# Where a scan batch routes its tokens: one batch later, or within the same batch

## The chip, the cores and the metric

The kernel runs on one core of a Trainium2 chip. The metric is the device time of one execution in microseconds (us), the median of several runs. Five engines work side by side, each through its own queue in a fixed order: PE (TensorE, matrix products), DVE (VectorE), ACT (ScalarE), POOL (GpSimd) and SP (SyncE, which here only issues transfers). An instruction whose input is not ready holds up all that stands behind it in its queue. Data move between the chip's memory (HBM) and the on-chip memory (SBUF) by DMA transfers; PE writes to PSUM, of which there are eight banks.

## The reference, cut to what matters

The input x has 8 batches of 512 tokens of 256 numbers each. Four layers follow one another, each added to x: a scan layer, a mixture of experts, an attention layer, and the same mixture again. The change touches the scan layer and the first mixture:

```python
xi = silu(x @ Win + bin_)                 # scan layer, x normalised
h = h * 0.9 + xt[:, :, None] * Bp         # a state for each channel, token after token
y = einsum('bij,ji->bi', h, Cp) + Dp * xt
x = x + y @ Wout + bout
...
scores = sigmoid(x @ router_w.T)          # mixture, x normalised again, 16 experts
# of four groups of four experts the best two by their two best scores; then the best four experts
tw = tw / tw.sum() * 2.5
x = x + sum of tw * expert(x) over the four experts + shared_expert(x)
```

## The kernel before, in words

Everything is float32. The work has four stages: the **scan stretch** (scan layer, routing and the shared part of the first mixture, `stretch(Scan())`, L1489), the routed experts of the first mixture (`routed`, L1494), the attention stretch with the second mixture's routing and shared part (`stretch(Attention())`, L1498), and the second mixture's routed experts (L1567). Between the two kinds of stage lies memory: routing sends each token's normalised row, with its four expert numbers and weights, to four places of a sorted table `xg` in HBM, and the routed stage reads that table block by block.

In a stretch, batch b of the layer runs beside other work for other batches: the routing of batch b-1 (its x is final when its layer is done), the rest of the routing of batch b-2, the shared experts of batch b-2, and the norm and transposes of batch b+1. The batches are the steps of the loop at L1410; batch 0 has its own start (`first_two`, L1387).

For the scan layer, `main` (L521) works through four **columns** of 128 channels. For each: four PE instructions into `pz_s` (L529), a sigmoid on ACT (L538), a product on DVE (L539), the scan on DVE (L541), a product with Dp on ACT (L542), a sum on DVE (L545). Then come four tiles of the output projection `py_s` on PE (L483), which DVE adds to x in pairs (L492). The shared experts (L1045) give four pairs of products `pg_m` (L1060), each with a sigmoid on ACT (L1078) and two products on DVE (L1079, L1080), and then sums `pd_m` (L1089).

The **routing** of a batch (class `Route`, L579, and `choices`, L650) is a chain through all engines:

- norm: statistics on DVE (L441, L442), the reciprocal root on POOL (L461), the normalised rows on DVE (L466), written into a tile `sorted_m` of which there are two. An `iota` on POOL (L591) writes token numbers into it. In the scan stretch the rows of a route stand behind the last weights (L741) of the route before it (`past`, L601).
- scores: transposes on PE into `pt_m` (L403), copies on ACT to `xT_m` (L405), products with the router's weights `pl_m` (L627), a transpose on DVE (L638), a sigmoid on ACT (L642).
- choices, five steps on DVE (L652 to L697, a chain of small instructions): the best groups, the best four experts, and a table `sel_m` of them.
- prefix products: `sel_m` times a triangle and times ones on PE into `pr_m` (L705, L706), which count how many earlier tokens chose each expert; DVE adds the counts of earlier batches (L708, L710, L716).
- places: DVE picks the four places of each token (L722, L728); then the weights (the same lines on the scores, L738 to L741).
- scatters: 16 indirect transfers on POOL (L755), each of which sends 128 rows of the tile to their places. ACT casts the places to whole numbers two scatters at a time (L752), pinned behind what ACT was given before.

**The order.** Each piece of work is a generator that yields between its steps. `beside` (L346) merges pieces: it always advances the one that is least far along, as a share of its own length. `timed` (L362) gives a piece that has no length of its own a list of **places**, one for each step, as shares of the batch (0 its start, 1 its end). The result is the program's order. The compiler's scheduler then builds each engine's queue from it: among the instructions that it takes to be ready, the one that comes first in the program's order goes first. In the trace PE's queue follows the places: batches 3 to 6 have the same order of products.

The places of the scan stretch (L500) are, for the routing of batch b-1 within batch b: norm statistics 0.08 to 0.2, rows 0.32 to 0.4, transposes at 0.48 and 0.52, logits from 0.61, choices 0.71 to 0.97. Its prefix products, places and weights come in batch b+1 at 0.1, 0.14 and 0.18, its 16 scatters there from 0.22 to 0.86 (L1427). The last batch of the loop (batch 7, L1432 to L1443) has a list of its own, in which route 6 goes as far as its first four scatters (`SENT`), beside the 16 scatters of route 5 (0.22 to 0.66). Route 7 is worked out behind the loop (L1467 to L1477), beside the other 12 scatters of route 6, and its last scatters with the block tables behind that.

Of the kernel before, what the change touches and what calls it, by code (L numbers as in the profile page):

```python
# [19 lines left out]
NT = T // P  # L20
# [11 lines left out]
EG, TKG, TK = 4, 2, 4  # L32
# [29 lines left out]
SENT = 4  # L62
# [6 lines left out]
PICKS = 5  # L69
# [11 lines left out]
def tile_hybrid_block(  # L81
# [67 lines left out]
    def rows_of(part, b: int):  # L149
        return part[b * T : (b + 1) * T, :].rearrange("(t p) d -> p t d", p=P)  # L150
# [57 lines left out]
    def load_shared():  # L208
        nc.sync.dma_start(out=sg_sb, in_=sh_gate_w.rearrange("(p k) f -> p k f", p=P))
        nc.sync.dma_start(out=su_sb, in_=sh_up_w.rearrange("(p k) f -> p k f", p=P))  # L210
        nc.sync.dma_start(out=sd_sb, in_=sh_down_w.rearrange("(k p) d -> p k d", p=P))
# [150 lines left out]
    def timed(steps, *places):  # L362


        def scaled():
            now = 0
            for place in places:
                yield place - now
                now = place
                next(steps)  # L370
            for _ in steps:
                pass

        return Piece(1, scaled())

    def spread(first: float, last: float, many: int):
        return [first + (last - first) * k / many for k in range(many)]

    def some(steps, many: int):

        for _ in range(many):
            yield next(steps)

    def issue(piece):
        for _ in piece.steps:
            pass
# [85 lines left out]
    def kb4(name: str):  # L472
        return work.tile([P, NT, D], FP, tag="kb4", name=name, bufs=KB)
# [21 lines left out]
    class Scan:  # L495
# [1 line left out]
        early = 0  # L497


        norms, scores, choose = (0.08, 0.2, 0.32, 0.4), (0.48, 0.52, 0.61, 0.66), (0.71, 0.97)  # L500
        last_rows, last_scores = (0.26, 0.33), (0.43, 0.46)

        def load(self, b: int):
# [611 lines left out]
    class Attention:  # L1115
        mixture, ahead, copies, turns = 1, 2, by_both, (0.65, 0.85)
        early = 2
        norms, scores, choose = (0.0, 0.12, 0.2, 0.28), (0.29, 0.45, 0.55, 0.6), (0.66, 0.95)
        last_rows, last_scores = (0.2, 0.28), (0.35, 0.38)

        def end(self):
# [222 lines left out]
    def stretch(layer):  # L1344


        i = layer.mixture
        xT, xn, made, routes, sends = {}, {}, {}, {}, []

        def norm(b: int, first: bool = False):  # L1350
            def place():
                xn[b] = kb4(f"xn_{i}_{b}")
                return xn[b]

            return normed(b, f"l{i}_{b}", place, first, first)

        def turn(b: int, copies=layer.copies):
            if i == 1 and b >= layer.ahead:
                return by_shares(lambda: xn.pop(b), f"l{i}_{b}", lambda xnT: xT.update({b: xnT}), True)
            return turned(lambda: xn.pop(b), f"l{i}_{b}", lambda xnT: xT.update({b: xnT}), copies)  # L1360

        def project(b: int):
            made[b], piece = layer.project(b, xT.pop(b))
            return piece

        def store(b: int):
            nc.sync.dma_start(out=rows_of(parts[i][0], b), in_=x_tiles[b])

        def experts(b: int):
            return shared_experts(i, b, lambda: routes.pop(b).held["xnT"], i == 1)  # L1370

        for b in range(layer.ahead):
            if b < layer.early:
                if b in unturned:
                    issue(Piece(0, unturned.pop(b)))
                xT[b] = ready.pop(b)
            else:
                layer.load(b)
                first = i == 0 and b == 0
                issue(Piece(0, norm(b, first)))  # L1380
                issue(Piece(0, turn(b, by_both if first else layer.copies)))
                if first:
                    load_shared()
            if b == 0:
                issue(project(b))

        def first_two():  # L1387

            layer.load(1)
            issue(Piece(0, norm(1, True)))  # L1390
            for _ in range(2):
                pending.pop(0)()
            main = layer.main(0, made.pop(0))
            issue(Piece(0, some(main.steps, NI)))
            issue(Piece(0, turn(1)))
            issue(project(1))
            second = layer.main(1, made.pop(1))
            issue(Piece(0, some(second.steps, NI)))
            issue(main)
            return Piece(second.columns - NI * KD * T, second.steps)  # L1400

        def start_route(b: int):
            routes[b] = Route(i, b, layer.copies)
            store(b)
            return routes[b]

        begun = None
        if layer.mixture == 0:
            begun = first_two()
        for b in range(1 if begun else 0, B):  # L1410
            pieces = [begun or layer.main(b, made.pop(b))]
            begun = None
            nxt, last = b + layer.ahead, b == B - 1
            fill = []
            if layer.ahead > 1 and not last:
                fill.append(project(b + 1))
            if b > 1:
                shared_sum = experts(b - 2)
                if last:

                    each = shared_sum.columns // 12
                    rest = Piece((12 - HELD) * each, shared_sum.steps)

                    many = HELD * each if layer.mixture else HELD * each * 3 // 2
                    shared_sum = Piece(many, some(shared_sum.steps, HELD))
                fill.append(shared_sum)
                pieces.append(timed(sends.pop(), 0.1, 0.14, 0.18, *spread(0.22, 0.66 if last else 0.86, NT * TK)))  # L1427
            if fill:
                pieces.append(behind(*fill))
            if b > 0:  # L1430
                r = start_route(b - 1)
                if last:  # L1432
                    pieces.append(timed(r.norm(), *spread(0.0, 0.12, NT), *spread(*layer.last_rows, NT)))
                else:
                    first, then, rows, full = layer.norms
                    pieces.append(timed(r.norm(), *spread(first, then, NT), *spread(rows, full, NT)))
                sends.append(r.rest)
                if last:
                    pieces += [
                        timed(r.scores(), *layer.last_scores, *spread(0.5, 0.56, NT)),  # L1440
                        timed(some(r.rest, PICKS), *spread(0.57, 0.67, PICKS - 1), 0.76),
                        timed(some(r.rest, 3 + SENT), 0.79, 0.81, 0.83, *spread(0.85, 1.0, SENT)),
                    ]  # L1443
                else:
                    pieces += [
                        timed(r.scores(i == 1), *layer.scores[:2], *spread(*layer.scores[2:], NT)),
                        timed(some(r.rest, PICKS), *spread(*layer.choose, PICKS)),
                    ]
            if nxt < B:
                added = layer.load(nxt)  # L1450
                if added is not None:
                    pieces.append(timed(added, 0.24, 0.28))
                pieces += [
                    timed(norm(nxt), *spread(0.32, 0.44, NT), *spread(0.56, 0.64, NT)),
                    timed(turn(nxt), *layer.turns),
                ]
            issue(beside(*pieces))
            if layer.ahead == 1 and nxt < B:
                issue(project(nxt))
            if i == 0 and b == 2:  # L1460
                for make in pending:
                    make()
        layer.end()

        r = start_route(B - 1)  # L1467
        chain = 3 + PICKS
        issue(
            beside(  # L1470
                behind(rest, experts(B - 2)),
                timed(r.norm(by_vector=True), *spread(0.0, 0.05, 2 * NT)),
                timed(sends.pop(), *spread(0.0, 0.5, NT * TK - SENT)),
                timed(r.scores(), 0.2, 0.22, *spread(0.28, 0.33, NT)),
                timed(some(r.rest, chain + 8), *spread(0.36, 0.68, chain), *spread(0.7, 1.0, 8)),
            )
        )  # L1477
        table = []
        issue(
            beside(  # L1480
                experts(B - 1),
                timed(r.rest, *spread(0.0, 0.5, NT * TK - 8)),
                timed(blocks(i, table), 0.03, 0.14, 0.26, 0.38),
            )
        )
        return table

    with banks_of(one=8):
        table = stretch(Scan())  # L1489
        wqkv_sb, wo_sb = load_attention_weights()  # L1490
# [136 lines left out]
```

## Time and profile before

| | us |
|---|---|
| median of 10 runs | 1686.69 |
| lowest and highest run | 1680.57, 1690.44 |
| the profiled execution | 1694.76 |
| its span, first to last instruction | 1693.0 |
| busy PE, DVE, ACT, POOL in the span | 1607.1, 1163.4, 750.2, 758.9 |
| scan stretch, batches 2 to 7 of its loop | 59.5 to about 300 |
| its tail, up to the last shared-expert product | to 351.4 |

The profile is of one execution. Batch b of the scan stretch can be found by its first products `pz_s`: batch 2 starts at 59.5 us, batch 3 at 101.8, batch 4 at 140.8, batch 5 at 179.9, batch 6 at 218.9, batch 7 at 257.9. In a timeline line the columns are start, duration, engine, source line, operation, output<-inputs, shapes and count; a bracket at the end is the time for which the engine was idle before, and what ended it. Names have their numbers left out: `sorted_m` is that of any route. A matmul in float32 shows as two records.

### The profile page before, as it was taken

What the parts mean: (1) busy time and instruction counts of PE and PEld (TensorE: products, weight loads), DVE (VectorE), ACT (ScalarE), POOL (GpSimd) and SP (SyncE); (2) the same over time, 40 slices, a digit from 0 to 9 for tenths busy, and PEclk for the clock granted to TensorE, in tenths of its full rate; (3) what the DMA queues carried; (4) which work ended last, traced back from release to release, by engine and by line L of the source; (5) the groups of instructions that cost most, each with busy time, mean ns of one, the idle gap of its engine ahead of it and who ended that gap; (6) DMA issues with size and microseconds to landing.
All of it is one profiled execution on the core that took longest, in us unless ns stands there. A gap on an engine that the chain in (4) does not pass through costs nothing.

```text
span 1693.0 us, 34302 instructions
## 1 busy us (share of the span) xinstructions
PE 1607.1 (95%) x9996; PEld 1162.2 (69%) x9996; DVE 1163.4 (69%) x3693; ACT 750.2 (44%) x1494; POOL 758.9 (45%) x656
## 2 busy tenths in 40 slices
PE   6899998999999999999999999999999999999993
PEld 3566665589999999963344444444457999999993
DVE  7888888545666766647887877877754766666662
ACT  3232232135555555544544344344314555555551
POOL 3355555635554655530031431422452555455563
PEclk8999999999999999999999999999999999999997
DMA  5345423547776776541324234232544777677776
GB/s 164 121 162 178 147 86 104 192 95 105 107 103 102 109 103 102 75 79 38 88 80 122 90 92 123 78 101 71 171 169 94 109 103 101 102 133 125 126 128 180
DMA packets 278382, 192.95 MB, mean 114 GB/s; under 512 B 166992, under 2 KB 259952, under 8 KB 278192
## 3 DMA queue, kind: packets, MB, share of 16 engines
q1 hardware_dynamic: 224528, 114.68, 26.9%
q0 software_dynamic: 51984, 72.09, 23.9%
q10 hardware_dynamic: 1680, 3.93, 0.6%
q8 instruction: 85, 1.39, 0.4%
q14 instruction: 105, 0.86, 0.2%
HBM read 87.36 MB, written 103.23 MB: 113 GB/s over the span
## 4 chain that ended last, share of the span: by engine, by line
PE 39%; DVE 7%; DMA 3%; issue 2%; POOL 1%; ACT 0%; SPq 0%; DVEq 0%; POOLq 0%; ACTq 0%
PE ph L953 15%; PE pyr L984 7%; PE ps_a L1198 4%; PE pg_m L1060 3%; PE po_a L1233 3%; PE pd_m L1089 2%; PE pq_a L1143 2%; PE pv_a L1161 2%; PE py_a L483 1%; POOL xg L755 1%; DMA part<-rows 1%; DMA xg<-sorted_m,slots_m 1%; DVE w_all L1212 1%; DVE w_all L1220 1%; DMA sum<-part 1%
## 5 line engine op out<-in xcount | busy, mean ns | idle before, releaser
L994 POOL DMA_INDIRECT part<-rows x272 | 425.5, 1564 | 358.0 <-ACT rows L993 213.5
L755 POOL DMA_INDIRECT xg<-sorted_m,slots_m x256 | 259.5, 1014 | 310.9 <-issue 76.0
L953 PEld LDWEIGHTS ph<-rows,gate 128*128 128x128 f32 x2160 | 279.9, 192 | 29.3 <-ACT rows L936 18.8
L953 PE MATMUL ph<-rows,gate 128*128 128x128 f32 x2160 | 292.4, 279 | 0.0
L953 PE MATMUL ph<-rows,up 128*128 128x128 f32 x2160 | 285.9, 275 | 0.0
L984 PE MATMUL pyr<-w_all,rows 128*128 x1088 | 278.9, 380 | 0.0
L926 DVE COPY up<-w_all 128x512 f32 x270 | 119.1, 442 | 219.0 <-PE ph L953 202.2
L953 PEld LDWEIGHTS ph<-rows,up 128*128 128x128 f32 x2160 | 263.7, 193 | 0.0
L926 ACT COPY gate<-w_all 128x512 f32 x270 | 166.3, 618 | 115.6 <-PE ph L953 108.6
L984 PEld LDWEIGHTS pyr<-w_all,rows 128*128 128x128 f32 x1088 | 187.0, 192 | 14.4
L993 ACT ACTIVATE rows<-pyr,gain 128x256 f32<-128x256 f32 x272 | 128.7, 473 | 80.8 <-PE pyr L984 61.0
L961 ACT ACTIVATE rows<-ph 128x256 f32<-128x256 f32 x272 | 104.3, 384 | 123.4 <-PE ph L953 106.7
L1209 ACT ACTIVATE w_all<-ps_a 128x1024 f32<-128x1024 f32 x128 | 124.4, 1020 | 54.3 <-PE ps_a L1198 51.1
L963 DVE TENSOR_TENSOR rows<-ph,rows 128x256 f32<-128x256 f32 x272 | 115.1, 423 | 45.4 <-ACT rows L961 41.2
L1198 PE MATMUL ps_a<-w_all 32*128 32x384 f32 (+3 forms) x1024 | 125.5, 483 | 9.5 <-ACT w_all L1209 8.7
L964 DVE TENSOR_TENSOR rows<-ph,rows 128x256 f32<-128x256 f32 x272 | 115.3, 424 | 26.3 <-PE ph L953 1.7
L1060 PE MATMUL pg_m<-xT_m,su_sb 128*128 128x512 f32 x256 | 125.4, 612 | 0.0
L1089 PE MATMUL pd_m<-sd_sb,act_m 128*128 128x256 f32 x512 | 122.2, 383 | 2.8 <-DVE act_m L1076 2.0
L1060 PE MATMUL pg_m<-xT_m,sg_sb 128*128 128x512 f32 x256 | 123.6, 606 | 0.0
L1089 PEld LDWEIGHTS pd_m<-sd_sb,act_m 128*128 128x128 f32 x512 | 95.4, 190 | 28.0 <-issue 6.7
L1198 PEld LDWEIGHTS ps_a<-w_all 32*128 32x128 f32 x1024 | 49.6, 190 | 78.3 <-issue 29.9
L1060 PEld LDWEIGHTS pg_m<-xT_m,sg_sb 128*128 128x128 f32 x256 | 47.4, 194 | 58.6 <-issue 50.4
(222 smaller groups left out, 2067.5 us busy)
## 6 DMA issues: line engine op xcount, KB each, us to landing
rows<-xg SPq DMA_DIRECT2D x712, 32.0 KB
rows<-xg SPq DMA_DIRECT2D x94, 134.0 KB
part<-x SPq DMA_DIRECT2D x16, 512.0 KB
part<-ys_m SPq DMA_DIRECT2D x14, 512.0 KB
sum<-part SPq DMA_DIRECT2D x13, 512.0 KB
w_all<-in_L_ffn_gate_w_dram SPq DMA_DIRECT2D x24, 256.0 KB
w_all<-in_L_ffn_up_w_dram SPq DMA_DIRECT2D x24, 256.0 KB
w_all<-in_L_ffn_down_w_dram SPq DMA_DIRECT2D x24, 256.0 KB
```

Of the source, the lines that this page charges most:

```text
L755: nc.gpsimd.indirect_dma_start(out=xg[i], out_offset=bass.IndirectOffsetOnAxis(ap=slots[:, at : at + 1], axis=0), in_=rows[:, t, :], in_of ...
L926: copy(here, w_all[:, bass.ds(held[n][0] + half * KD * F, KD * F)])
L953: nc.tensor.matmul(ph[s][:, f * P : (f + 1) * P], lhsT=both[s][:, k * F + f * P : k * F + (f + 1) * P], rhs=rows[:, ROW + k * P : ROW + (k ...
L963: nc.vector.tensor_mul(act, ph[0], act)
L964: made = nc.vector.tensor_mul(act, ph[1], act)
L984: nc.tensor.matmul(py, lhsT=act[:, f * P : (f + 1) * P], rhs=w_all[:, bass.ds(w + 2 * KD * F + f * D, D)], start=(f == 0), stop=(f == KF - 1),
L993: nc.scalar.mul(y, py, gain[:, TK : TK + 1])
L994: nc.gpsimd.indirect_dma_start(out=parts[i][n % 2], out_offset=bass.IndirectOffsetOnAxis(ap=rows[:, D + 2 * TK : D + 2 * TK + 1].bitcast(U ...
L1060: made = nc.tensor.matmul(dst, lhsT=w[:, k, f * P : (f + 1) * P], rhs=xnT[:, k, :], start=(k == 0), stop=(k == KD - 1),)
L1089: nc.tensor.matmul(py[:, j, :], lhsT=acts[n][:, f, t * P : (t + 1) * P], rhs=shared[n][3][:, f, :], start=(n == 0 and f == 0), stop=(n == ...
L1198: nc.tensor.matmul(ps[j // 2][:, j % 2, col : col + n], lhsT=k_sb[w][r, o, c * P : (c + 1) * P], rhs=q_sb[r, o, c * P : T], start=True, st ...
L1209: nc.scalar.activation(es[two], ps[two][:, :, 0:cols], AF.Exp, scale=ATT_SCALE)
```

## The change

The routing of batch b-1 is moved forward within batch b, and three more steps of it and four scatters are put into that batch. The last batch of the loop, the work behind the loop and the attention stretch keep their places; in the last batch only what is left of route 5 changes.

| step of route b-1 | before | after |
|---|---|---|
| norm statistics | 0.08 to 0.2 | 0.0 to 0.12 |
| rows | 0.32 to 0.4 | 0.2 to 0.28 |
| transposes | 0.48, 0.52 | 0.34, 0.38 |
| logits | 0.61 to 0.66 | 0.46 to 0.51 |
| choices | 0.71 to 0.97 | 0.56 to 0.76 |
| prefix products, places, weights | 0.1, 0.14, 0.18 of batch b+1 | 0.8, 0.83, 0.86 |
| scatters 1 to 4 | 0.22 to 0.38 of batch b+1 | 0.9 to 1.0 |
| scatters 5 to 16 | 0.38 to 0.86 of batch b+1 | 0.0 to 0.6 of batch b+1 |

Where batch b+1 is the last, its scatters ran from 0.22 to 0.66 before, and the remaining 12 run from 0.0 to 0.45 after.

```diff
-        norms, scores, choose = (0.08, 0.2, 0.32, 0.4), (0.48, 0.52, 0.61, 0.66), (0.71, 0.97)
+        norms, scores, choose = (0.0, 0.12, 0.2, 0.28), (0.34, 0.38, 0.46, 0.51), (0.56, 0.76)
+        places, sends, rest = (0.8, 0.83, 0.86), (0.9, 1.0, SENT), (0.0, 0.45, 0.6)
...
+        places, sends, rest = (), (0.0, 0.0, 0), (0.22, 0.66, 0.86)
...
-                pieces.append(timed(sends.pop(), 0.1, 0.14, 0.18, *spread(0.22, 0.66 if last else 0.86, NT * TK)))
+                first, end, full = layer.rest
+                first_steps = () if layer.places else (0.1, 0.14, 0.18)
+                left = NT * TK - layer.sends[-1]
+                pieces.append(timed(sends.pop(), *first_steps, *spread(first, end if last else full, left)))
...
-                        timed(some(r.rest, PICKS), *spread(*layer.choose, PICKS)),
+                        timed(
+                            some(r.rest, PICKS + len(layer.places) + layer.sends[-1]),
+                            *spread(*layer.choose, PICKS),
+                            *layer.places,
+                            *spread(*layer.sends) if layer.places else (),
+                        ),
```

The second `places, sends, rest` line is the attention layer's, which keeps what it had.

## The prediction

> **What bounds the kernel now.** I read the windows view first, cut at the batches of the scan stretch (the first line is batch 2, then 3, 6, 7 and the tail). Columns: stretch, then busy time of PE, weight loads, DVE, ACT and POOL, the granted clock, DMA share and GB/s.
>
> ```profile
> 59.50:101.80 42.30, 40.16 (x149) 24.74 (x149) 35.78 (x125) 11.26 (x26) 21.15 (x23) 0.96 0.45 155
> 101.80:140.80 39.00, 38.16 (x149) 24.07 (x148) 34.43 (x113) 11.96 (x27) 20.36 (x23) 1.00 0.45 156
> 218.90:257.90 39.00, 38.16 (x149) 24.07 (x148) 31.42 (x87) 11.97 (x27) 22.04 (x24) 1.00 0.24 84
> 257.90:300.00 42.10, 35.11 (x129) 20.19 (x128) 32.58 (x112) 10.76 (x29) 22.64 (x25) 1.00 0.40 133
> 300.00:351.40 51.40, 51.27 (x196) 31.40 (x196) 24.14 (x86) 9.38 (x20) 26.73 (x28) 1.00 0.46 151
> ```
>
> PE bounds the stretch: batches 3 to 6 take 39.0 us for 38.2 us of matmuls. Only 0.84 us a batch is to be had there, 2.1 in batch 2, 7.0 in batch 7. The waits of PE from 59.5 to 300 us say for what (total, times, longest):
>
> ```profile
> PE pt_m L403 <- DVE sorted_m L466: 6.1, 7, 1.1
> PE pr_m L705 <- DVE sel_m L697: 3.5, 1, 3.5
> PE pl_m L627 <- ACT xT_m L405: 1.4, 1, 1.4
> ```
>
> All are the routing that the change moves. The pt_m waits are 1.09 and 1.05 us in batch 2, 0.84 in each of batches 3 to 6, 0.64 in batch 7; the other two are batch 7's. The timelines of batch 7 and after:
>
> ```profile
> 272.91 1.03 PE L403 MATMUL pt_m<-ident,sorted_m 128*128 128x128 f32 x3 [0.64 <-DVE sorted_m L466]
> 277.65 0.43 PE L627 MATMUL pl_m<-xT_m,rw_sb 128*32 128x128 f32 x8 [1.41 <-ACT xT_m L405]
> 287.47 0.43 PE L705 MATMUL pr_m<-sel_m,tri 128*128 128x64 f32 x2 [3.47 <-DVE sel_m L697]
> 300.00 1.82 PE L403 MATMUL pt_m<-ident,sorted_m 128*128 128x128 f32 x8 [1.48 <-DVE sorted_m L466]
> ```
> ```profile
> 276.31 0.72 ACT L542 ACTIVATE xi_s<-xi_s,d_sb 128x512 f32<-128x512 f32 x1 [3.08 <-DVE state_s L541]
> 277.02 0.57 ACT L405 COPY xT_m<-pt_m 128x512 f32<-128x512 f32 x1
> ```
> ```profile
> 273.35 1.05 POOL L755 DMA_INDIRECT xg<-sorted_m,slots_m  x1 [11.79 <-ACT slots_m L752]
> ...
> 292.56 0.97 POOL L755 DMA_INDIRECT xg<-sorted_m,slots_m  x1 [0.30 <-DVE x L492]
> ```
> ```profile
> 299.50 1.41 DVE L466 TENSOR_SCALAR sorted_m<-x,mv_m,rstd_m 128x256 f32<-128x256 f32 x4 [2.74 <-DMA xg<-sorted_m,slots_m]
> ```
>
> The reader is to see two chains. The transposed copies stand in ACT's queue behind the product of column 3, which waits for DVE's scan. And route 5's 16 scatters start 15 us late and run to 293.5 us; their landing holds the tile that route 7's rows need, so PE waits until 300.0.
>
> **What is moved.** For routes 0 to 5: the prefix products (4 PE records, 0.4 us), 14 DVE instructions of L708 to L741 (batch 4's rows sum to 3.4 us), 2 of 8 casts on ACT (0.18 each) and 4 of 16 scatters (0.96 plus 0.30 of issue each on POOL) go ahead of the batch's end; the other 12 scatters start at 0. Nothing is added. No SP instruction moves. Norms, transposes, logits and choices go 0.12 to 0.2 of a batch forward within it. Work on each engine is the same, so only waits can change.
>
> **Batch 7 and tail.** (1) The 3.4 us of route 5's DVE work, at 264.0 to 272.2 in this trace, is gone. The rows of route 6, which had to follow its last instruction, come at about 269 and the 0.64 wait goes. (2) The scan of column 3, ended at 276.3, is then held by its own chain alone: products done 270.4, sigmoid 0.9, L539 0.7, scan 1.1, so 273.1. The copies no longer stand behind it, PE gets to pl_m at 275.6 rather than 276.2, and the 1.41 goes. (3) The 3.47 stays: from pl_m's end (279.5) to sel_m's (287.4) DVE runs a chain of 7.9 us, which starts 2.05 earlier, as PE does. (4) Twelve scatters at 1.27 from 257.9 end at 273, landed (2.7 median, 6.5 longest) by 280. Route 7's rows then wait for their rstd alone, 296.8 - 2.05 = 294.7, are done by 296.2, and PE's sum products before them end at 298.5 - 2.05 = 296.5: the 1.48 goes. Sum: 0.64 + 1.41 + 1.48 = **3.5 us off**. What is late next: from 300 to 351 PE is idle for 0.13 us, and everything behind hangs on PE; route 7's scatters (321 to 341.8) follow that route's chain and move with it. Bounds: 7.0 if the 3.47 goes too, 1.5 if only the landing does.
>
> **Batches 3 to 6.** I lay out a new batch with the start-to-start times of the rows (a column of pz_s or half pair of pg_m 1.72, a tile of py_s or pd_m 1.73, half of pt_m 0.47, pl_m 0.57, pr_m 0.4), t from the batch's start, in order of the places: pt_m at 15.5, xT wanted for pl_m at 18.1, pr_m at 31.7 (place 0.8 ties with the third tile of py_s, which goes first), end at 38.2. The rows no longer follow a gain of the same batch; rstd comes by 2.7 (L460 ends 0.4 into batch 5, a scatter may be ahead for 1.27, the power takes 1.04), so they are done by 8 to 10, between columns 0 and 1, and the 0.84 goes. But the transposes stand 3.1 us nearer to column 3: its products end at 13.7, its scan at 16.7, the product L542 at 17.5, so a copy behind it ends at 18.1 to 18.7. I take 0.5 us of new wait at pl_m; 0 if the copies stand in front, 1.4 (batch 7's row) if DVE is late again. At pr_m: pl_m ends at 19.2, sel_m followed 10.0 us later in batch 5 (205.8 to 215.8), one pair of shared experts (1.25) now falls into that chain, so 30.5, before 31.7: nothing, 3.47 (batch 7's row) at worst. After pr_m, DVE has 3.4 + 0.6 + 1.4 us for 6.5 of PE, so gains are ready about at the batch's end; casts and scatters wait for nothing longer than that. Their POOL queue then holds rstd for one scatter at most (1.27), which the 15.5 of pt_m hides; without that cover PE would wait the same 1.27. Sum per batch -0.84 + 0.5 = -0.3; **four batches, 1.2 us off**, from 3.4 off to 16 on.
>
> **Batches 1 and 2.** DVE, not PE, bounds these: it is hardly idle from 53.8 to 82.4. Route 0's 3.4 us now stand in front of batch 2's columns instead of between them, so the sum up to column 3's scan (end 79.4) is the same, and 1.0 more with three rows pulled in front: 80.4. Behind it stand L542 (0.8) and a copy (0.6), so pl_m starts at about 82.0, while PE is there at 59.5 + 18.1 + 0.4 = 78.0. The 2.14 of pt_m go, 4.0 at pl_m come. Then pl_m and two half pairs (0.57 + 3.43) bring PE to the first py_s at 86.0; it was 86.3. If the copies stand in front of the product, py_s starts at 82.1, when column 3 is done: 4.2 off. pr_m in batch 1, if it is queued ahead of batch 2's columns, stops PE up to 5 us for sel_m (64.6), most of it under DVE's work: 1.5 on at most. I take **0**, from 4.2 off to 3.2 on (1.5 + 1.7, next).
>
> Clock: in batch 2 the granted clock reads 0.50 at 82 to 84 us after the waits of 1.09 and 1.05; four matmuls of pg_m take 3.24 there against 1.88. With pt_m's second half that is 1.70 us. After batch 7's 3.47 the clock stays 1.00. I keep the 1.70 in batch 2, as a wait stays there. [...]
>
> **The sum.** -3.5 - 1.2 + 0 = -4.7 us on the profiled execution's 1694.8 (span 1693.0 and 1.8 around it): 1690.1. That execution is 8 us above the median of the runs, 1686.7; I carry the difference over: **1682.0**. A measurement can tell about 0.2% (3.4 us) from no change.
>
> **Rivals.**
> - All waits of batches 2 to 6 go and none comes: 4 x 0.84 + 2.14 + 1.70 + 3.5 = 10.7 off, 1676.0. For it: DVE is idle for 4.6 us (39.0 - 34.4) or more in batches 3 to 6. Against: up to column 3 of batch 2 it has next to none.
> - Slower: PE stops at pr_m and pl_m in batches 2 to 6, since both now follow close behind what they need in queues that are fixed. For it: batch 7 already has choices and pr_m in one batch, and pays 3.47 and 1.41. Against: there PE has few other products between them. It decides where the chain from pl_m to sel_m is over 12.5 us, or column 3's scan over 1 us late. At 1.5 us for each wait: 5 x (3.0 - 0.84) = 10.8 on, less 3.5: 7.3 on, 1694.0.
> - It does not do what it says, or the gain is eaten: the compiler's order goes by what it takes to be ready, so the queues may hardly change, or the 3.5 are lost at the first block of the routed stage, where PE waits 0.92 and 1.70 and the clock is 0.50 from 356 to 359. About 1 off, 1685.7.
>
> **How the numbers follow.** Forecast 0.46 (own range 1679 to 1685.5; 0.36 of it faster by over 0.2%, 0.10 within); all waits go 0.14 (faster); eaten 0.14 (within); slower 0.26 (0.21 over 0.2%, 0.05 within). Together 0.50, 0.29, 0.21. Range 1675 to 1694: it takes in both outer rivals; batches 3 to 6 at their worst lie outside.
>
> **What would show it.** Right: route 5's last scatter of the loop near 273 us on the old time scale, no DMA in front of route 7's rows, no pt_m wait in batches 3 to 6, a short one at pl_m, a long one at pl_m in batch 2, pr_m unwaited except in batch 7. Wrong: waits at pr_m in every batch, batches over 39.0 us, or a tail that starts as late as before.

## The result, and the profile after

The changed kernel takes **1707.3 us** (median of 17 runs, 1701.99 to 1713.09), the kernel before 1688.0 us (median of 62 runs, 1680.57 to 1698.69): a ratio of 1.0116, 95% interval 1.0104 to 1.0128. The change makes the kernel 19 us slower, where I forecast 4.7 us faster; the time lies outside the range.

The profiled execution of the changed kernel took 1705.3 us; its span of 1703.6 is 10.6 us above that of before. The execution profiled of before is 7 us above its median and that of after 2 us below, so the two profiles show only a part of the 19 us. Up to the end of the tail the changed kernel is 15.0 us later (366.4 against 351.4 us). Of these 15.0 us, 13.7 are left at the first product of the attention stretch (748.9 against 735.3), 11.5 at the last routed stage's first (1294.9 against 1283.4) and 10.6 at the end. The change touches none of these later stages, and no run here shows why they are shorter in this execution.

The windows view of the changed kernel, cut at its own batches: 2, 3, 4, 6, 7 and the tail. Columns as in the prediction: stretch, then length, busy time of PE, weight loads, DVE, ACT and POOL, the granted clock, DMA share and GB/s.

```profile
63.40:102.86 39.46, 39.08 (x150) 24.43 (x150) 35.73 (x107) 11.59 (x28) 22.07 (x21) 0.97 0.38 134
102.86:145.05 42.19, 39.02 (x149) 24.32 (x148) 34.02 (x114) 11.65 (x27) 23.16 (x24) 0.96 0.44 149
145.05:185.73 40.68, 37.80 (x149) 23.86 (x148) 33.09 (x96) 11.67 (x27) 21.94 (x24) 1.00 0.39 136
226.42:269.80 43.38, 40.54 (x150) 24.89 (x148) 31.07 (x88) 11.67 (x27) 22.04 (x24) 0.92 0.22 75
269.80:315.81 46.01, 38.48 (x125) 22.61 (x124) 31.30 (x100) 10.25 (x27) 24.66 (x26) 0.89 0.34 115
315.81:366.40 50.59, 50.46 (x197) 31.06 (x195) 23.32 (x84) 9.38 (x20) 24.77 (x25) 1.00 0.47 155
```

Batch 2 starts 3.9 us later than before (63.4 against 59.5) and is 2.8 shorter; batches 3 to 6 took 39.0 each and take 42.2, 40.7, 40.7 and 43.4; batch 7 is 3.9 longer, the tail 0.8 shorter. Sum: 3.9 - 2.8 + 10.8 + 3.9 - 0.8 = 15.0. The first term depends on the execution: a1 and a3 below, whose order on PE is the same up to there, have the same wait of 4.6 us, but start batch 2 at 66.4 and 64.9. At 50 to 55 us, at the end of batch 1, the clock reads 1.00 in the changed kernel's profile and 0.66 in that of before; two records of py_s take 0.60 us there in the changed kernel, and 1.06 in a1.

The waits of PE in the changed kernel from 55 to 330 us (total, times, longest):

```profile
PE pl_m L628 <- ACT xT_m L405: 16.0, 6, 4.1
PE pr_m L706 <- DVE sel_m L698: 8.1, 2, 4.6
```

The pt_m waits, 7.6 us in 8 places before, are gone, as the prediction said. In their place PE waits 16.0 us for transposed copies, once in each of batches 2 to 7, and 4.6 more for a selection. The places of the two, and batch 7 and the tail that answer to the prediction's lines (timeline of PE: start, duration, engine, line, operation, output<-inputs, elements, count, and in brackets the idle time before it and what ended it):

```profile
62.53 0.66 PE L706 MATMUL pr_m<-sel_m,tri 128*128 128x64 f32 x2 [4.61 <-DVE sel_m L698]
...
63.41 3.15 PE L530 MATMUL pz_s<-xT_l,w_scan 128*128 128x512 f32 x4
```
```profile
290.40 0.43 PE L628 MATMUL pl_m<-xT_m,rw_sb 128*32 128x128 f32 x8 [4.06 <-ACT xT_m L405]
...
301.80 0.69 PE L706 MATMUL pr_m<-sel_m,tri 128*128 128x64 f32 x2 [3.47 <-DVE sel_m L698]
...
315.81 1.10 PE L403 MATMUL pt_m<-ident,sorted_m 128*128 128x128 f32 x8
```

The first is route 0's prefix product at the end of batch 1: 4.61 us of nothing, then batch 2's first column, at a clock that reads 0.50 from 63.4 to 65.4 us (3.15 us against 1.88). In batch 7 the pl_m wait has grown from 1.41 to 4.06 and the 3.47 at pr_m is unchanged; in the tail the 1.48 before route 7's transposes is gone.

**Where the 2.8 us of every batch come from.** In the kernel before, batch 4 starts at 140.83. There too a scatter stands ahead of the power that makes rstd, but the power ends 1.9 us into the batch, column 0 starts 2.6 into it, and the rows come only at 157.65, after the weights (POOL, then DVE):

```profile
140.73 0.96 POOL L755 DMA_INDIRECT xg<-sorted_m,slots_m  x1 [0.30 <-issue]
141.71 1.05 POOL L461 TENSOR_TENSOR rstd_m<-rstd_m,neg_half 128x4 f32<-128x4 f32 x1
```
```profile
143.47 0.75 DVE L539 SCALAR_TENSOR_TENSOR xi_s<-pz_s,b_in_sb,xi_s 128x512 f32<-128x512 f32 x1 [2.19 <-ACT xi_s L538]
```

In the changed kernel batch 4 starts at 145.05. Its chain, followed back from pl_m, on PE, ACT, DVE and POOL:

```profile
166.14 0.92 PE L628 MATMUL pl_m<-xT_m,rw_sb 128*32 128x128 f32 x16 [2.82 <-ACT xT_m L405]
```
```profile
146.97 0.69 ACT L539 ACTIVATE xi_s<-pz_s,b_in_sb 128x512 f32<-128x512 f32 x1 [1.13 <-PE pz_s L530]
...
164.81 0.72 ACT L543 ACTIVATE xi_s<-xi_s,d_sb 128x512 f32<-128x512 f32 x1 [2.17 <-DVE state_s L542]
165.43 0.18 ACT L753 CAST slots_m<-choices_wm 128x2 uint32<-128x2 f32 x1
165.51 1.06 ACT L405 COPY xT_m<-pt_m 128x512 f32<-128x512 f32 x2
```
```profile
145.34 0.16 DVE L460 TENSOR_SCALAR rstd_l<-mv_l 128x4 f32<-128x4 f32 x1
149.98 1.38 DVE L466 TENSOR_SCALAR sorted_m<-x,mv_m,rstd_m 128x256 f32<-128x256 f32 x4 [4.49 <-DMA xg<-sorted_m,slots_m]
151.28 0.74 DVE L540 SCALAR_TENSOR_TENSOR xi_s<-pz_s,b_in_sb,xi_s 128x512 f32<-128x512 f32 x1
```
```profile
144.10 0.99 POOL L756 DMA_INDIRECT xg<-sorted_m,slots_m  x1 [9.54 <-DVE sorted_m L742]
145.39 0.96 POOL L756 DMA_INDIRECT xg<-sorted_m,slots_m  x1 [0.30 <-issue]
146.66 0.96 POOL L756 DMA_INDIRECT xg<-sorted_m,slots_m  x1 [0.30 <-issue]
147.93 0.96 POOL L756 DMA_INDIRECT xg<-sorted_m,slots_m  x1 [0.30 <-issue]
148.91 1.04 POOL L461 TENSOR_TENSOR rstd_m<-rstd_m,neg_half 128x4 f32<-128x4 f32 x1
```

Read it from the bottom. The four scatters of route 2, which the change put at the end of batch 3, start when its weights (L742) are there, at 144.1, and stand in POOL's queue ahead of the power that makes route 3's rstd; each takes 1.27 us, so the power ends at 149.95, 4.9 us into the batch. Route 3's rows (L466) start 0.03 later. They stand in DVE's queue **ahead of column 0** (L540), whose products end at 146.9 and whose sigmoid (ACT L539) ends at 147.7: DVE idles 4.49 us, and column 0 starts 6.2 us after the batch, where it started 2.6 after it before. The whole column chain of DVE is 3.6 us late, so column 3's scan ends at 164.8, ACT's product L543 follows, the copies follow that, and PE waits. The label of the DVE wait names a DMA; the power's end says otherwise, and so does the tile: the scatters of 144 to 149 read route 2's, and the last one out of the tile that route 3 writes was issued at 131.5. This had to be tried.

**The theory** to test, then: scatters ahead of the power in POOL's queue, together with rows ahead of column 0 in DVE's, cost the batches 3 to 7; the prefix product ahead of batch 2 costs the start. **Rivals**: the transposes at 0.34 and 0.38 are too near to column 3's product whatever DVE does; the prefix products and places cost in the same batch; the label is right and the landing of scatters holds the rows, through the tile they are read from.

### The profile page after: what moved, and what is told of

It reads as the page before. It is cut to its first block, busy times and chain, and to the rows that moved or that the text cites. A ratio compares the mean times of both kernels' runs of the same rounds, so it can differ in the third digit from the quotient of the medians.

```text
span 1703.6 us, 34320 instructions
## 1 busy us (share of the span) xinstructions
PE 1607.8 (94%) x9996; PEld 1162.1 (68%) x9996; DVE 1164.0 (68%) x3693; ACT 749.3 (44%) x1494; POOL 765.0 (45%) x656
## 4 chain that ended last, share of the span: by engine, by line
PE 40%; DVE 7%; DMA 3%; issue 2%; POOL 1%; ACT 1%; ACTq 0%; POOLq 0%; SPq 0%; DVEq 0%
PE ph L954 15%; PE pyr L985 7%; PE ps_a L1200 4%; PE pg_m L1061 3%; PE po_a L1235 3%; PE pd_m L1090 2%; PE pq_a L1145 2%; PE pv_a L1163 1%; PE py_a L483 1%; DMA xg<-sorted_m,slots_m 1%; POOL xg L756 1%; DVE w_all L1214 1%; DVE w_all L1222 1%; PE pt L936 1%; DMA part<-rows 1%
## 5 line engine op out<-in xcount | busy, mean ns | idle before, releaser
L756 POOL DMA_INDIRECT xg<-sorted_m,slots_m x256 | 266.8, 1042 | 336.5 <-ACT slots_m L753 83.4
L1061 PE MATMUL pg_m<-xT_m,su_sb 128*128 128x512 f32 x256 | 129.2, 627 | 0.0
```

What stands on the lines that cost most here:

```text
L756: nc.gpsimd.indirect_dma_start(out=xg[i], out_offset=bass.IndirectOffsetOnAxis(ap=slots[:, at : at + 1], axis=0), in_=rows[:, t, :], in_of ...
L1061: made = nc.tensor.matmul(dst, lhsT=w[:, k, f * P : (f + 1) * P], rhs=xnT[:, k, :], start=(k == 0), stop=(k == KD - 1),)
```

## The experiments

All ratios are to the kernel before, run beside them; the changed kernel's is 1.0116. Differences in us to the changed kernel are worked out from these ratios and carry their intervals, some 3 us either way.

**No scatter in the same batch** (a1): `places, sends, rest = (0.8, 0.83, 0.86), (0.9, 1.0, 0), (0.22, 0.66, 0.86)`.

> The changed kernel with all 16 scatters of a route back in the following batch (from 0.22 on); norms, scores, choices, prefix products and places stay where the change put them. Theory (four scatters of 1.27 us each stand in POOL's queue ahead of the power that makes the next route's rstd, and DVE's rows stand ahead of column 0): DVE's wait before the rows of 3.4 to 4.6 us in batches 3 to 7 falls to about 1.3, the pl_m wait of 2.8 to 4.1 there falls below 0.5, batches 3 to 6 take 38.2 to 39.0 us in place of 40.7 to 43.4, and the kernel is 12 to 18 us faster than the changed one, within 0.3% of the kernel before. Rival (the transposes at 0.34 and 0.38 are simply too near to column 3's product in ACT's queue): the pl_m waits stay at 2 or more and the time stays within 4 us of the changed kernel's. Rival (prefix products and places in the same batch cost it): no change either.

Ratio 1.0054 (1.0036 to 1.0073), so 10 us faster than the changed kernel: over half of the loss hangs on the place of four scatters. pl_m waits: 1.97, 0.38, 1.72, 1.72 and 0.86 in batches 3 to 7; batches 3 to 6 take 41.6, 38.3, 39.7 and 41.4. In batch 4 DVE waits 1.16 us before the rows and PE 0.38, with transposes and places just where the change has them: neither can be what costs 2.8 there. The gain is smaller than I expected in batches 3, 5 and 6. In batches 5 and 6 the landing rival holds (batch 3's rows carry the same label). Batch 5 of this kernel (start 186.54), POOL and DVE:

```profile
187.81 1.04 POOL L461 TENSOR_TENSOR rstd_m<-rstd_m,neg_half 128x4 f32<-128x4 f32 x1 [0.46 <-DVE rstd_l L460]
190.39 0.15 POOL L592 IOTA sorted_m<- 128x16 int32 x1 [1.53 <-DMA xg<-sorted_m,slots_m]
```
```profile
190.38 1.38 DVE L466 TENSOR_SCALAR sorted_m<-x,mv_m,rstd_m 128x256 f32<-128x256 f32 x4 [2.64 <-DMA xg<-sorted_m,slots_m]
```

Here the power is done at 188.85 and the rows still wait until 190.38, as does the iota that writes the same tile: the last scatter out of that tile was issued at 186.40 and had not landed. So the same label stands for two causes, and only the neighbour's end tells which.

**rstd on DVE** (a2): in the branch of the routes that aren't last, `r.norm(by_vector=i == 0)`.

> The changed kernel with rstd of routes 0 to 5 worked out on DVE (3 Newton steps, 12 small instructions, some 1.0 us more DVE work a batch) in place of POOL's power; the four scatters stay at the end of the batch. Theory (POOL's queue holds rstd): the rows no longer wait, column 0's first DVE instruction comes 2.5 to 4 us after the batch's start in place of 6.2, the pl_m waits fall below 1.0 and the kernel is 8 to 16 us faster than the changed one. Rival (the label of the wait is right: the scatters' landing, or the reuse of the tile of rows, holds the rows): the rows still wait some 4 us in each of batches 3 to 7 and the time stays. Rival (transposes too near to column 3): pl_m waits stay at 2 or more.

Ratio 1.0038 (1.0013 to 1.0063), 13 us faster than the changed kernel. The scatters stay where the change put them, and yet:

```profile
150.33 0.73 DVE L466 TENSOR_SCALAR sorted_m<-x,mv_m,rstd_m 128x256 f32<-128x256 f32 x2 [0.24 <-DMA xg<-sorted_m,slots_m]
150.98 0.75 DVE L540 SCALAR_TENSOR_TENSOR xi_s<-pz_s,b_in_sb,xi_s 128x512 f32<-128x512 f32 x1
```

The wait is 0.24 us (batch 4, start 147.5). Batches 3 to 6 take 39.3, 38.2, 38.6 and 38.3, with a pl_m wait of 1.44 left in batch 3; batch 7, whose route keeps the power on POOL, keeps its pl_m wait (4.04). It was the power's place in POOL's queue, not the landing.

**Rows behind column 0** (a3): scatters and power stay as the change has them; DVE alone is reordered, for routes 1 to 5.

```
-            past = (lambda: gained.get(self.b - 1)) if self.i == 0 else lambda: None
+            past = (lambda: summed[0]) if self.i == 0 and 0 < self.b < B - 2 else (...)
```

(`summed` holds the instructions L546 of the running batch; ... is the old expression.)

> The changed kernel with one order added on DVE: the rows of routes 1 to 5 follow column 0's sum. Scatters stay ahead of the power. Theory: the late rstd then holds nothing, since the rows are wanted at 15 us of the batch; column 0 starts at 2.6 us, pl_m waits 0 to 1 us in batches 3 to 6, which take 38.2 to 39.5 us; 8 to 14 us faster than the changed kernel (route 6 keeps its old order, so batch 7 keeps its waits). Rival (transposes too near to column 3): the 1.4 us of rows now stand between columns 0 and 1, column 3 is as late as before, pl_m waits stay at 2 or more, within 4 us of the changed kernel.

Ratio 1.0023 (1.0000 to 1.0046), 16 us faster than the changed kernel. Batch 4 of this kernel (start 144.27), POOL, DVE and PE:

```profile
148.12 1.64 POOL L461 TENSOR_TENSOR rstd_m<-rstd_m,neg_half 128x4 f32<-128x4 f32 x1
```
```profile
146.91 0.75 DVE L541 SCALAR_TENSOR_TENSOR xi_s<-pz_s,b_in_sb,xi_s 128x512 f32<-128x512 f32 x1 [2.19 <-ACT xi_s L540]
...
150.98 1.38 DVE L466 TENSOR_SCALAR sorted_m<-x,mv_m,rstd_m 128x256 f32<-128x256 f32 x4
```
```profile
163.07 0.91 PE L633 MATMUL pl_m<-xT_m,rw_sb 128*32 128x128 f32 x16 [0.53 <-ACT xT_m L405]
```

The power is as late as in the changed kernel (it ends at 149.76, 5.5 us into the batch) and costs nothing: column 0 starts 2.64 us after the batch, the rows fill the time after its sum, and batches 3 to 6 take 38.4 us each, less than before. The pl_m wait is 0.53. In the program only the order of two groups on DVE separates this from the change.

**Places alone** (a4): norm and transposes at their old places, prefix products, places and four scatters in the same batch.

```
norms, scores, choose = (0.08, 0.2, 0.32, 0.4), (0.48, 0.52, 0.57, 0.61), (0.66, 0.88)
places, sends, rest = (0.9, 0.92, 0.94), (0.96, 1.0, SENT), (0.0, 0.45, 0.6)
```

> Only one part of the change: prefix products, places and (some) scatters come at the end of the same batch (0.9 to 1.0), while the routing norm and transposes have their old places (0.32/0.40, 0.48/0.52), and logits and choices nearly so (0.57 to 0.88). Theory: rows no longer follow a gain of the same batch, the transposes stand 5 us further behind column 3 than in the change, so pt_m and pl_m do not wait in batches 3 to 6: 38.2 to 39 us each, 12 to 20 us faster than the changed kernel; pr_m may wait, as it is close behind the choices: up to 3 us a batch. Rival (prefix products and places in the same batch are what costs): waits at pr_m of 3 us or more in every batch, and the time at or above the changed kernel's.

Ratio 1.0052 (1.0030 to 1.0074), 11 us faster than the changed kernel. Batches 4 to 6 take 37.8 us, with no wait of PE over 0.3 us, none at pr_m: prefix products in the same batch cost nothing there. Batch 3 takes 47.3: this is the one place where the compiler put eight scatters ahead of a power. DVE in that batch (start 105.5):

```profile
113.30 0.75 DVE L540 SCALAR_TENSOR_TENSOR xi_s<-pz_s,b_in_sb,xi_s 128x512 f32<-128x512 f32 x1
121.82 0.41 DVE L466 TENSOR_SCALAR sorted_m<-x,mv_m,rstd_m 128x256 f32<-128x256 f32 x1 [7.78 <-POOL rstd_m L461]
122.16 1.21 DVE L542 TENSOR_TENSOR_SCAN state_s<-decay,xi_s 128x512 f32<-128x512 f32 x1
```

The rows now stand ahead of column 1's scan and hold it for 7.78 us; here the label does name the power. It ended in 5.38 us at pl_m.

**Eight scatters** (c1): `sends = (0.9, 1.0, 8)` in the changed kernel.

> The changed kernel with eight scatters in place of four at the end of the same batch (the other eight in the next). Theory (each scatter ahead of the power holds the next route's rows by its 1.27 us): the power of rstd comes 5.1 us later, DVE's wait before the rows grows from 4.5 to some 9 us in batches 3 to 7 (less by what DVE does between, if column 0 is put between the rows), pl_m waits grow by 2 to 5 us each, 10 to 25 us slower than the changed kernel, ratio to the kernel before 1.017 to 1.026. Rival (the scatters' place in POOL's queue does not matter): ratio as of the changed kernel, 1.010 to 1.013.

Ratio 1.0195 (1.0158 to 1.0233). Batch 4 of this kernel (start 152.6), POOL and DVE:

```profile
161.53 1.04 POOL L461 TENSOR_TENSOR rstd_m<-rstd_m,neg_half 128x4 f32<-128x4 f32 x1
```
```profile
162.61 0.41 DVE L466 TENSOR_SCALAR sorted_m<-x,mv_m,rstd_m 128x256 f32<-128x256 f32 x1 [9.53 <-POOL rstd_m L461]
```

The ratio is of four runs, beside a kernel before that took 1708.2 us. Four more scatters make the wait 9.53 - 4.49 = 5.04 us longer, 1.26 each: the step of a scatter on POOL. pl_m waits grow from 2.8 to 7.5, and the four matmuls behind the waits of batches 3 to 5 take 3.78 us each time, against 1.98 in batches 4 and 5 of the changed kernel; batches 3 to 6 take 47.8 each.

**Route 0 late** (b1): the change for routes 1 to 5, but route 0's prefix products, places and all scatters in batch 2.

```
+                early = layer.places and b > 2
+                if not early:
+                    first, end, full = (0.22, 0.66, 0.86)
```

> The changed kernel, but route 0 keeps its prefix products, places and 16 scatters in batch 2; routes 1 to 5 as changed. Theory (the prefix products of route 0 stand on PE between batch 1 and batch 2's first columns and wait 4.6 us there for the selection, and the clock is 0.50 after that): the pr_m wait of batch 1 goes, batch 2 starts at about 59.5 us in place of 63.4 to 67.9; the pt_m waits of 2 us come back in batch 2, which takes 42 to 44 us in place of 39.5 to 41. Net 1 to 5 us faster than the changed kernel, with the pl_m waits of batches 3 to 7 unchanged. Rival (batch 1's stretch is bound by DVE, so the wait is only moved): batch 3 starts as late as in the changed kernel, 102.9 us or later, no gain.

Ratio 1.0104 (1.0070 to 1.0138), which can't be told from the changed kernel's. Batch 2 starts at 59.5 and batch 3 at 99.7, where the changed kernel's started at 102.9 and before's at 101.8: the stop at the prefix product does cost, 3.2 us by this pair of profiles (it would be more against a1 or a3, which start batch 3 at 106.6 and 105.9). But batch 3 then takes 46.3 us. Its POOL queue holds six scatters behind the bias sums and ahead of the power (two of route 0, four of route 1), rows wait 5.51 us and pl_m 6.54. The gain went into the first cause.

**Both repairs** (b2): a3's order for routes 1 to 6, and route 0 late.

> The changed kernel with both repairs: the rows of routes 1 to 6 follow column 0's sum on DVE, and route 0 keeps its places and scatters in batch 2. Theory: batches 3 to 6 take 38.4 us each as with the first repair alone, batch 2 starts at 59.5, batch 7's pl_m wait of 4.0 falls below 1, its pr_m wait of 3.47 stays. Sum against the kernel before: batches 3 to 6 2.6 us less, batch 2 0 to 2 less, batch 7 and the tail 1 to 3 less: 3 to 7 us faster than before, ratio 0.996 to 0.998. Rival (the route's part in batch 1 is bound by DVE anyway): as the rows alone, ratio 1.001 to 1.003.

Ratio 0.9986 (0.9964 to 1.0009): with the two causes taken away, as far as they are, the whole 1.16% is gone. It is not the gain I expected, since batch 3 takes 43.8: its six scatters end at 108.8, so that rows placed behind column 0 still wait 3.87 us there, ahead of column 1. Batches 4 to 6 take 38.4.

**Places in the same batch, scatters in the next, route 0 late** (b3): `norms, scores, choose` as in a4; `places, sends, rest = (0.9, 0.92, 0.94), (0.96, 1.0, 0), (0.1, 0.5, 0.66)`.

> Prefix products and places of routes 1 to 5 in the same batch (0.9 to 0.94), all 16 scatters in the next one (0.1 to 0.66), routing norm and transposes at the old places, route 0 wholly as before. Theory: no scatter is ahead of the power of the next route, so no rows wait as in the places-alone kernel's batch 3 (7.8 us behind eight scatters), and batches 3 to 6 take 37.8 to 38.4 us; batch 2 starts at 59.5; 3 to 8 us faster than the kernel before, ratio 0.995 to 0.998. Rival (prefix products and places cost in the same batch): pr_m or pl_m waits of 1 us or more in batches 3 to 6, ratio 1.00 or above.

Ratio **0.9952 (0.9929 to 0.9975)**, the fastest of all: 8 us under the kernel before. Its windows, batches 2 to 5:

```profile
59.48:102.50 43.02, 40.90 (x153) 25.04 (x152) 38.31 (x130) 11.27 (x26) 21.13 (x23) 0.96 0.44 156
102.50:141.30 38.80, 37.88 (x149) 23.92 (x148) 32.23 (x114) 11.57 (x27) 21.75 (x23) 1.00 0.47 161
141.30:179.20 37.90, 37.90 (x150) 23.96 (x150) 30.90 (x96) 11.78 (x27) 21.87 (x23) 1.00 0.43 146
179.20:217.00 37.80, 37.80 (x149) 23.92 (x148) 30.82 (x95) 11.77 (x27) 21.87 (x23) 1.00 0.42 145
```

PE is busy for the whole of batches 4 and 5.

**Norm and scores alone** (b4): the change's first line with `places, sends, rest = (), (0.0, 0.0, 0), (0.22, 0.66, 0.86)`.

> The other part alone: routing norm, transposes, logits and choices at their new, earlier places, but prefix products, places and scatters of each route in the next batch, as before. Theory: the rows follow the weights of the route before on DVE, which come only at some 12 to 14 us of the batch, while the transposes are wanted 5.5 us earlier than before: pt_m or pl_m waits of 2 to 6 us in batches 2 to 6, 41 to 45 us a batch, at or above the changed kernel's time (ratio 1.010 to 1.020); no pr_m wait in batch 1. Rival (the weights come early enough): batches 3 to 6 at 39 us, ratio within 0.998 to 1.004.

A miss: ratio 0.9970 (0.9948 to 0.9993), faster than before. Batch 2 takes 39.7 and batches 3 to 6 38.7. Batch 4 (start 138.5), PE:

```profile
154.55 1.39 PE L403 MATMUL pt_m<-ident,sorted_m 128*128 128x128 f32 x6
156.19 0.50 PE L403 MATMUL pt_m<-ident,sorted_m 128*128 128x128 f32 x2 [0.25 <-DVE sorted_m L466]
156.53 1.88 PE L1061 MATMUL pg_m<-xT_m,su_sb 128*128 128x512 f32 x4
158.34 0.65 PE L628 MATMUL pl_m<-xT_m,rw_sb 128*32 128x128 f32 x16
```

Route 2's weights are done 15.7 us after the start of the batch, later than the 12 to 14 I expected. But the transposes are wanted at 16.0, which is 1.6 earlier than before (17.6 in batch 5) and not 5.5. So the rows are nearly in time. And with the transposes at the change's very places pl_m waits for nothing: the copies stand in front of column 3's product here. The places alone do not cost, then; what is left of that rival is the 0.5 us at pl_m that a3 shows where the copies stand behind the product.

**Three more combinations**, beside the same kernel before of 1708.2 us as c1. Their PE shows gaps, most of 0.2 to 1.7 us, that no releaser explains, so beside the ratios only batches without such gaps are read. c2 is a1 with a3's order and route 0 late; c3 is b3 with a3's order for routes 1 to 6; c4 is b3 with the change's first line for route 1 alone.

> Norms, scores, choices, prefix products and places of routes 1 to 5 where the change put them; no scatter in the same batch (all 16 from 0.22 of the next on); rows of routes 1 to 5 behind column 0's sum on DVE; route 0 keeps its places in batch 2. Theory: no scatter ahead of the power, no row ahead of column 0, no prefix product in batch 1, so none of the three costs is left: batch 2 starts at 59.5 us, batches 3 to 6 take 37.9 to 38.5 us, 5 to 10 us faster than the kernel before, ratio 0.994 to 0.997. Rival (the transposes at 0.34 and 0.38 are too near to column 3's product, even with DVE in time): pl_m waits of 0.5 to 2 us in each batch and ratio 0.998 to 1.002.

> The places-with-scatters-next kernel (ratio 0.9952) with the rows of routes 1 to 6 behind column 0's sum on DVE as well. Theory: there the rows waited for nothing in batches 3 to 6, so these stay at 37.8 to 38.0 us; the order can only help in batch 2, where the rows of route 1 follow the weights of route 0: the pt_m waits of 1.07 and 1.05 and the slow clock after them (1.5) may go, 0 to 3.5 us. Ratio 0.993 to 0.996. Rival: the rows now delay column 1 by 1.4 us, pl_m waits 0.5 in each batch, ratio 0.996 to 0.998.

> The places-with-scatters-next kernel (ratio 0.9952), with the norm, transposes, logits and choices of route 1 alone (batch 2) at the change's earlier places. Theory: batch 2 takes about 39.7 us, as in the kernel with norm and scores alone, in place of 43.0, since the compiler then puts route 0's weights earlier; the rest as it was; ratio 0.992 to 0.995. Rival: batch 3 pays for it, as it did when route 0 was late in the changed kernel (46.3): ratio 0.996 or above.

c2: 0.9981 (0.9961 to 1.0000); c3: 0.9966 (0.9941 to 0.9991); c4: 0.9994 (0.9975 to 1.0014). c2 has the theory's 38.5 us in batches 4 to 6, but the rival's 0.5 at pl_m and its ratio, and 43.7 in batch 3. c3 can't be told from b3 by these intervals, and c4's gain does not show in the ratio. None beats b3.

## Why the prediction was wrong

**The step that failed** is in batches 3 to 6: "Their POOL queue then holds rstd for one scatter at most (1.27), which the 15.5 of pt_m hides", and the rows "are done by 8 to 10, between columns 0 and 1". Both halves are wrong. Four scatters stand ahead of the power, not one, since all four wait for the same weights (ready at 143.2, 1.8 us before batch 4) and come together at the batch's end: rstd comes at 4.9 in place of 2.7. The rows are done even earlier than I said, at 6.3, but ahead of column 0 and not behind it. And the cover was the wrong one: I asked when PE wants the rows and not what stands behind them on DVE. Once the rows no longer had to follow a weight of the same batch, the compiler put them ahead of column 0; a late rstd then holds all of DVE's columns. The runs: without the scatters ahead (a1), without the power on POOL (a2), or with the rows behind column 0 (a3), 10 to 16 of the 19 us come back; with twice the scatters (c1) the wait doubles.

The rest of that step was right. I laid out L542's product at 17.5 us of the batch and 0.5 at pl_m; a3, in which DVE is in time, has them at 17.47 and 0.53, with batches 0.6 us shorter than before (I said 0.3). pr_m in batches 2 to 6 waited for nothing, as said. Measured for the four batches: 10.8 on in place of 1.2 off; the bound I gave, 16 on, held it, but I left that end out of the range.

**Batches 1 and 2.** I put the pr_m of batch 1 at "1.5 on at most". It stops PE for 4.61 us, with 1.3 of slow clock behind it, and batch 2 starts 3.9 later; the 4.0 I expected at pl_m in batch 2 is 0.32. Together 1.1 on, where I said 0: two wrong terms that nearly cancel, and by luck, as a1 and a3, with the same order on PE up to there, start batch 3 late by 4.8 and 4.1 us. That the stop is not merely hidden under DVE's work shows in b1.

**Batch 7 and the tail.** (1) the 0.64 is gone; (3) the 3.47 stays; (4) the 1.48 is gone, and route 7's rows wait for their rstd alone: right. But the way to (4) is not as I laid it out: route 5's remaining 12 scatters wait 4.34 us for ACT's casts behind the power and end at 296.2, 26.4 us into the batch (284 on the old time scale), not at 273. That is still early enough, since route 7's rows start at 314.5. (2) is wrong by the same cause: pl_m waits 4.06, not 0, since route 5's four scatters hold route 6's power and rows (4.57 us on DVE). After (3) the clock read 0.50 from 302.7 to 306.7 us (the 16 matmuls of py_s take 6.38 us against 3.67), which I had excluded because it stayed at 1.00 in before's execution. Sum: 3.1 on in place of 3.5 off.

**The rivals.** The slower one named the right place, pl_m, and its condition, column 3's scan over 1 us late; it ended 19.7 us after the start, 3 later than I laid out. But it priced the wait at 1.5, had no reason for the delay, and expected waits at pr_m as well, which did not come in batches 2 to 6; so it stopped at 1694.0. "It does not do what it says" was wrong: the instructions stand where the change puts them.

## What to carry to other kernels

When a step is moved, look on each engine at what will stand *behind* it, not only at who wants its result: a cover of 15 us on PE is worth nothing if an engine that serves its queue in order, as DVE did here for 4.49 us, has the next column queued behind the waiting rows. The scatters that POOL issues counted as work on POOL here: 1.27 us each ahead of a 1.04 us operation on which the whole chain hangs. And a bound worked out in the text belongs in the range.

## What the hardware showed

The slow clock did not follow here from the length of the wait before it. In the changed kernel PE waits 2.82, 2.83 and 2.84 us at pl_m in batches 4, 5 and 6. After the first two the clock stays at 1.00; after the third it reads 0.50, and the four matmuls that took 1.98 us take 3.78:

```profile
247.53 1.14 PE L628 MATMUL pl_m<-xT_m,rw_sb 128*32 128x128 f32 x16 [2.84 <-ACT xT_m L405]
248.61 3.78 PE L1061 MATMUL pg_m<-xT_m,sg_sb 128*128 128x512 f32 x4
252.18 2.58 PE L1061 MATMUL pg_m<-xT_m,su_sb 128*128 128x512 f32 x4
```

Batch 6 is 43.38 - 40.69 = 2.7 us longer than batch 5 for that alone. After batch 3's wait of 3.17 the clock is at 0.50 as well, for a shorter time (2.91 us for the same four). The 3.47 at pr_m in batch 7 had either outcome: clock 1.00 in the kernel before, 0.50 in the changed one.

Nor did only waits of about 3 us have slow clock behind them: in batch 2 of the kernel before, where PE ran nothing but transposes pt_m from 77.3 to 80.7 us, around waits of 1.09 and 1.05, the clock read 0.50 from 82 to 84. What decides it was not shown by any run here.

So a wait of about 3 us is priced at itself plus, some of the time, 2.7 (batch 6) or 3.1 (the 3.47 of batch 7: from the start of pr_m to the next pg_m 7.13 us, against 4.01 in the kernel before); how often is left open, as no run here isolates it.
